# A layer-normed time-mix scan and a GELU feed-forward: the first block's splits move behind the second term of W1

## The chip, the cores and the metric

The kernel runs on one core of one Trainium2 chip. Its time is the device time of one execution in microseconds (us). A profile records one execution: when every instruction began, how long it took and what ended the idle time before it. Engines are named as the profile names them: PE is the matmul engine (PEld its weight loads), DVE the vector engine, ACT the scalar engine, POOL the general one, SP the queue that issues nearly all transfers (DMAs).

## The reference

The input `x` has 4 sequences of 1024 tokens and 512 channels. Every token is layer-normed, and two branches are added to the residual.

```python
xn = layernorm(x)
xx = concat([xn[:, 1:2], xn[:, :-1]], axis=1) - xn       # the token before, minus this one
k = einsum('btc,hc->bth', xn + xx * time_mix_k, Wk)      # 704 hidden
r = einsum('btc,hc->bth', xn + xx * time_mix_r, Wr)
w = exp(-exp(time_decay))
state_t = state_{t-1} * w + relu(k_t);  out_t = state_t * r_t
out = einsum('bth,ch->btc', out, Wv)                     # back to 512 channels
out = layernorm(out) * ln_gamma + ln_beta
D = gelu(float16(xn) @ W0.T + bias0).astype(float16)     # 2048 hidden
E = float16(D @ W1.T + bias1)
result = x + out + E
```

## The kernel before

**Blocks and chunks.** The 4096 tokens are cut into eight blocks of 512 (`blocks`, index `i`; the blocks 0, 1, ... of this text are that index, so "block 2" of the change's name is `i == 1`). For each block, a loop over `n` goes through 16 chunks of 128 hidden units of the feed-forward. In chunk `n`, `up` multiplies W0's rows for a chunk two ahead (PSUM tile `pd`), ACT applies the GELU (line 876) and a cast (line 879), and `down` multiplies chunk `n`'s `d` by W1's rows into four accumulators `pe` (line 888), one for each 128 tokens.

**Pieces.** Between chunks PE does pieces of the other branch: `three_pass` multiplies one 128-wide slice `h` of k or r (tiles `pa` at line 695, `pb` at line 446), `half_pass` and `raw_halves` the last 64 hidden units, `out_piece` the product with Wv. A piece leaves a follower, the work that takes its result out of PSUM (for `three_pass`: ACT's line 707, DVE's line 708, and then the scan, line 587, or the gate, line 604). Followers run in the next chunk. All tiles `pd`, `pa`, `pb` and the like share one pool of four PSUM banks (`ps_mm`, function `bank`): a matmul group that opens a bank must wait until the tile that held it has been read out.

**Splits.** PE takes a product in several terms: an operand is split into a high part and remainders. `split` (lines 199 and 200) does so for W0 and W1: ACT writes the high term, DVE the second. `split_x` (lines 278, 333, 335, 337) does it for the mixer's inputs, `split_kr` (278, 285, 294, 295, 296) for Wk and Wr, and `split_wv` (278, 312, 315 to 317, or 321 and 322 for the last half slice) for Wv. In each of the last three DVE masks, ACT copies the mask's result and DVE makes the remainders. `split_kr` also appends three stores of 256 KB to `stores`, and `split` for W1 two; `store_weights` hands them to SP at the end of a chunk. Splits are done once, in block 0 and the start of block 1; later blocks load what was stored.

**Block 0.** Here W1's rows are split as well: `load_w1` at the end of each chunk splits the rows of two chunks on, into tiles that have two buffers for the high term and three for the second. r's first slice and all of k's are made unsplit before the loop; r's slices 1 to 4 are `three_pass` pieces in chunks 3, 5, 7 and 9, and need r's split input (`first_xr`) and Wr's split slices.

**What sets the order.** DVE, ACT, PE and SP issue in the order that is written out (`manual_schedule`). Work put down with `put(n, ...)` goes into `bg[n]`, in the order in which it is put, and `woven` runs it in chunk `n` beside the followers. In block 0 a chunk's end is this:

```python
woven(works, jobs + bg[n])
if i == 0:
    waiting.append((d, load_w1(*nxt)))
```

`turn` stands for the DVE transposes of the next block's input (line 380), `stats` and `norm_apply` for its norm (354 and 358), `rounded` (line 835) for reading the four `pe` tiles out at a block's end; the next block's first `down` waits for that.

Of the kernel before, what the change touches and what calls it, by code (L numbers as in the profile page):

```python
# [22 lines left out]
def time_mix_and_gelu_ffn(  # L23
# [40 lines left out]
    Q = 32  # L64
    QS = 62
    RAW_OUT = 1
    WV_FIRST = {0: 12, 1: 13, 2: 15, 3: 15, 5: 15}
    S = 4096.0
    WS = 4096.0
    MASK = -4096  # L70
# [177 lines left out]
    def load_w1(i, n):  # L248
        name = f"w1_{i}_{n}"
        if i == LAST and n >= NN - 2:  # L250
            w1 = [part(f"{name}_0"), pair(f"{name}_1")[0]]
        else:
            w1 = [
                part(f"{name}_0", tag="w1", bufs=2),
                part(f"{name}_1", F16, tag="w1l", bufs=3),
            ]
        if i == 0:
            split(*w1, w1_raw.pop(n))
        for p in range(2):
            sbuf, kept = as_stored(w1[p], p), as_stored(w1_dram[n][p], p)  # L260
            if i == 0:
                stores.append((kept, sbuf))
            else:
                nc.sync.dma_start(sbuf, kept)
        return w1
# [696 lines left out]
    with tc.manual_schedule(engines=engines):  # L962
        for i in range(len(blocks)):
            j = i + 1
            tail = 4 if i == LAST else 0
            by_columns = range(NS // 2, NS) if tail else ()
            pieces, bg, early = defaultdict(list), defaultdict(list), defaultdict(list)

            def put(n, fn, *args, **home):
                bg[n].append(lambda: fn(*args, **home) if home else fn(*args))  # L970
# [32 lines left out]
            if i == 0:  # L1003
                state["x"] = x_next
                piece(1, raw_halves, i)
                for h in range(1, NF):
                    piece(2 * h + 1, three_pass, i, 1, h)
                for c in range(NC):
                    put(2 + c - (c == 0), split_w0, 2, c)
                    put(c // 2, load_w0, 3, c)  # L1010
                    put(5 + c, split_w0, 3, c)
                put(1, stats, *range(NS))
                put(3, lambda: norm_apply(j, state["x"]))
                for c in range(NC):
                    put(c // 2, split_first_xr, c)
                for n, h in ((7, 2), (10, 0), (11, 1)):
                    put(n, split_kr, 1, 0, h, **OWN)
                for h in range(1, NF):
                    put(2 * h - 1, first_kr, h)
                put(4, turn, 0, 1)  # L1020
                put(5, turn, 1, 5)
                put(7, turn, 5, 10)
                put(8, turn, 10, 11)
                put(9, turn, 11, 16)
                put(9, load_late_constants)
                put(12, split_half)
                for g in range(NN // G):
                    put(11 + (g or NN // G), store_w0l, g)
                put(15, store_weights)
                mix_at = (11, 12, 13, 15)  # L1030
            else:
                order = [(0, h) for h in range(NF)] + [(1, h) for h in range(NF)]
                halves_ahead_of = (3 if i == LAST else NF, NF)
                for k, (kind, h) in enumerate(order):
                    for half in range(2):
                        if k == halves_ahead_of[half]:
                            piece(half_at[half], half_pass, i, half)
                    piece(full_at[k], three_pass, i, kind, h)
                    if (kind, h) not in made:
                        put({(0, 3): 1, (0, 4): 2, (1, 0): 4}[kind, h], fetch_kr, i, kind, h)  # L1040
                    elif k > 1:
                        put(full_at[k - 2], fetch_kr, i, kind, h)
                xr_at = {1: (2, 3, 4, 5), LAST: (1, 2, 2, 3)}.get(i, (2, 2, 3, 3))
                for c, n in enumerate(xr_at):
                    put(n, split_xr, i, c)
                if j <= LAST:
                    put(2, fetch_x)
                    for s in range(NS):
                        put(3 + s // 2 if i == 1 else 4, stats, s)
                    put(5, lambda: norm_apply(j, state["x"]))  # L1050
                    turns = (4, 4, 4, 4) if i == 1 else (4, 5, 4, 3)
                    for k in range(sum(turns)):
                        unit = next(n for n in range(4) if k < sum(turns[: n + 1]))
                        put(6 + unit, turn, k, k + 1)
                mix_at = (10, 12, 13, 14)
# [3 lines left out]
            if j <= LAST:  # L1059
                for c in range(NC):  # L1060
                    put((10, 10, 11, 12)[c], x16, j, c)
                for c, n in enumerate(mix_at):
                    early[n].append((j, c))
                    put(n, mixed, j, c)
                    put(n + (n == 10), split_xk, j, c)
                for h, n in {0: WV_FIRST, 1: {NF - 1: 2}}.get(i, {}).items():
                    put(n, split_wv, h)
                put(13, fetch_kr, j, 0, 0)
                put(14, fetch_kr, j, 0, 1)

            pe = [ps_e.tile([P, C], F32, tag="pe", name=f"pe_{i}_{s}") for s in range(NS)]
            for n in range(NN):
                ahead = n + AHEAD
                if ahead == NN and j <= LAST:
                    xf = next_xf
                nxt = (i, ahead) if ahead < NN else (j, ahead - NN)
                paired = i > 0 and n < NN - tail
                order = HIGH_FIRST if paired and n % 2 == 0 else LOW_FIRST
                end = lambda s: NN - tail if s in by_columns else NN
                products, gelu = up(*nxt) if nxt[0] <= LAST else (None, None)  # L1080

                def hidden(p):
                    if products:
                        products(p, order if paired else HIGH_FIRST)

                def outputs(p):
                    if n < NN - tail:
                        down(n, range(NS), *operands, p, order, end=end)

                if n < NN - tail:  # L1090
                    operands = waiting.pop(0)
                if not paired:
                    hidden(0)
                    hidden(1)
                elif n % 2 == 0:
                    hidden(0)
                else:
                    hidden(1)
                    outputs(1)
                    hidden(0)  # L1100
                works = [follow() for follow in followers]
                works = [w for w in works if next(w, works) is None]
                several(scaled_now, *early[n])
                if i == 0 or n == out_at[0] or (n > out_at[0] and i < RAW_OUT):
                    finished(*works)
                    works = []
                followers = []
                if behind_works:
                    waiting.append(behind_works.pop()())
                if gelu and not paired:  # L1110
                    d = gelu()
                if ahead + 1 == NN and j <= LAST:
                    next_xf = ffn_input(j)
                if not paired:
                    outputs(1)
                outputs(0)
                if gelu and i > 0:
                    w1 = load_w1(*nxt)
                    if not paired:
                        waiting.append((d, w1))  # L1120
                two_on = (i, ahead + 2) if ahead + 2 < NN else (j, ahead + 2 - NN)
                if two_on[0] <= LAST:
                    load_w0l(*two_on)
                jobs = [
                    lambda s=s: finish(i - 1, s, e16s[s])
                    for s in (2 * n, 2 * n + 1)
                    if s < len(e16s)
                ]
                for work, *args in pieces[n]:
                    followers.append(work(*args))  # L1130
                if i == 0 and ahead + 2 < NN:
                    load_w1_raw(ahead + 2)
                woven(works, jobs + bg[n])
                if i == 0:
                    waiting.append((d, load_w1(*nxt)))
                elif paired and n % 2 == 0:
                    hidden(1)
                    outputs(1)
                    behind_works.append(lambda gelu=gelu, w1=w1: (gelu(), w1))
                elif paired:  # L1140
                    waiting.append((gelu(), w1))
                store_weights()
# [66 lines left out]
```

## Time and profile before

| | us |
|---|---|
| median of 3 runs | 857.76 (857.33 to 857.89) |
| the profiled execution | 857.93 |
| its span, first to last instruction | 856.1 |
| PE busy in the span | 847.0 (99%) |
| DVE busy | 687.1 (80%) |
| ACT busy | 438.1 (51%) |
| mean granted PE clock | 0.999 |

The profiled execution lies 0.17 us over the median, and 1.8 us of it are outside the span. A row of the timeline gives the start, the length, the engine, the line, the tile written and read, and in brackets the idle time before it and what ended that. A length is longer than the distance to the next row where two instructions overlap: DVE's split instructions last 0.69 us and start 0.61 us apart. The list of waits gives, for an engine and a line, the total idle time, how often it happened, and the longest.

### The profile page before, as it was taken

The numbers are of one execution on the slowest core, as the hardware profiler recorded it, in microseconds if no ns is written. First come the engines' busy times: TensorE is split into PE (matmuls) and PEld (weight loads), VectorE is DVE, ScalarE is ACT, GpSimd is POOL, SyncE is SP. The second block draws the span as 40 slices with busy tenths as digits, with TensorE's granted clock in tenths as the row PEclk, the third lists the DMA queues.
The fourth block names the chain that finished last, engine by engine and source line by source line (L and its number), as shares of the span: only waits on it lengthen the run. The fifth ranks groups of instructions, "written<-read, shape, count | busy, mean of one in ns | idle before, by whom it ended". The sixth has DMA issues, their size and how long they took to land.

```text
span 856.1 us, 11350 instructions
## 1 busy us (share of the span) xinstructions
PE 847.0 (99%) x3772; PEld 595.2 (70%) x3772; DVE 687.1 (80%) x1130; ACT 438.1 (51%) x748; POOL 80.4 (9%) x145
## 2 busy tenths in 40 slices
PE   9999999999999999999999999999999999999998
PEld 8556646667767767667777667677777667676776
DVE  6789898999868988789786897778796897876446
ACT  5857665546534563445725455344653545634422
POOL 1210000000211001000021001100011200200012
PEclk9999999999999999999999999999999999999999
DMA  9756995745467544856358455594465755467513
GB/s 279 252 178 239 306 282 193 249 151 182 148 230 225 172 136 149 288 165 209 130 170 284 148 180 172 159 308 146 151 193 161 272 173 181 127 220 247 169 54 111
DMA packets 120902, 166.72 MB, mean 195 GB/s; under 512 B 21487, under 2 KB 57740, under 8 KB 120844
## 3 DMA queue, kind: packets, MB, share of 16 engines
q1 hardware_dynamic: 120396, 165.34, 60.4%
q8 instruction: 30, 0.49, 0.2%
q10 hardware_dynamic: 448, 0.66, 0.2%
q14 instruction: 28, 0.23, 0.1%
HBM read 141.31 MB, written 24.64 MB: 194 GB/s over the span
## 4 chain that ended last, share of the span: by engine, by line
PE 82%; DVE 7%; DMA 5%; ACT 2%; issue 2%; SPq 2%; DVEq 0%; ACTq 0%
PE pd L862 22%; PE pe L888 22%; PE pa L695 14%; PE oa L792 7%; PE pb L446 7%; PE ob L800 4%; PE ph L724 3%; DMA x<-in_L_attn_x 2%; PE ob L802 1%; DMA krd<-wt 1%; DMA w0raw<-in_L_ffn_W 1%; SPq L239 1%; DVE w0l L200 1%; DVE wd L285 1%; ACT w L199 1%
## 5 line engine op out<-in xcount | busy, mean ns | idle before, releaser
L888 PE MATMUL pe<-w,d 128*128 128x512 f32 (+1 forms) x1008 | 262.9, 389 | 3.8 <-DVE w L200 3.4
L862 PE MATMUL pd<-xf,w0h 128*128 128x512 f32 x512 | 150.8, 415 | 0.1
L862 PE MATMUL pd<-x,w0l 128*128 128x512 f16 x512 | 132.2, 381 | 0.0
L876 ACT ACTIVATE d<-pd,late_sb 128x512 f16<-128x512 f32 x128 | 87.2, 681 | 75.4 <-PE pe L888 47.4
L862 PEld LDWEIGHTS pd<-xf,w0h 128*128 128x128 f32 x512 | 96.2, 188 | 28.4 <-issue 2.8
L888 PEld LDWEIGHTS pe<-w,d 128*128 128x128 f32 x504 | 94.7, 188 | 23.6 <-DVE e L835 1.2
L708 DVE SCALAR_TENSOR_TENSOR y<-pb,a 128x512 f32<-128x512 f32 x74 | 50.9, 688 | 65.5 <-PE pb L446 54.8
L888 PEld LDWEIGHTS <-d 128*128 128x128 f16 x524 | 50.6, 98 | 64.1 <-issue 5.1
L862 PEld LDWEIGHTS <-w0l 128*128 128x128 f16 x512 | 44.1, 98 | 62.2 <-issue 16.1
L879 ACT CAST d<-d 128x512 fp32r<-128x512 f16 x128 | 79.4, 620 | 10.3 <-PE pe L888 6.3
L380 DVE STREAM_TRANSPOSE xnT<-x 32x512 f32<-32x512 f32 x112 | 78.6, 702 | 2.2
L707 ACT ACTIVATE a<-pa 128x512 f32<-128x512 f32 x74 | 44.1, 596 | 70.2 <-PE pa L695 70.2
L348 POOL TENSOR_SCALAR ry<-mvy 128x1 f32<-128x1 f32 x32 | 18.9, 591 | 460.5 <-DVE mvy L355 460.5
L792 PE MATMUL oa<-wv,hg 128*128 128x512 f32 x140 | 54.5, 389 | 0.0
L792 PE MATMUL oa<-wv,lg 128*128 128x512 f32 x140 | 54.5, 389 | 0.0
L695 PE MATMUL pa<-lr,kr 128*128 128x512 f32 x136 | 52.9, 389 | 0.0
L695 PE MATMUL pa<-hr,kr 128*128 128x512 f32 x136 | 52.9, 389 | 0.0
L695 PE MATMUL pa<-hk,kr 128*128 128x512 f32 x132 | 51.4, 390 | 0.0
L695 PE MATMUL pa<-lk,kr 128*128 128x512 f32 x132 | 51.4, 389 | 0.0
L710 ACT ACTIVATE y<-y 128x512 f32<-128x512 f32 x35 | 22.1, 631 | 53.7 <-DVE y L708 53.7
L333 ACT CAST hg<-ug 128x512 fp32r<-128x512 f32 x35 | 21.7, 620 | 37.1 <-DVE ug L278 37.1
L807 DVE SCALAR_TENSOR_TENSOR oy<-ob,oa 128x512 f32<-128x512 f32 x28 | 19.3, 688 | 25.8 <-PE ob L802 25.8
(175 smaller groups left out, 1411.2 us busy)
## 6 DMA issues: line engine op xcount, KB each, us to landing
kr<-krd SPq DMA_DIRECT2D x201, 256.0 KB, 4.4
w<-w1d SPq DMA_DIRECT2D x112, 256.0 KB, 2.8
w<-w1d SPq DMA_DIRECT2D x112, 128.0 KB, 2.7
w0l<-w0d SPq DMA_DIRECT2D x108, 128.0 KB, 3.5
xres<-in_L_attn_x SPq DMA_DIRECT2D x32, 256.0 KB, 4.7
x<-in_L_attn_x SPq DMA_DIRECT2D x31, 256.0 KB, 5.0
krd<-wt SPq DMA_DIRECT2D x30, 256.0 KB, 3.3
out<-xres SPq DMA_DIRECT2D x28, 256.0 KB, 3.6
```

Of the source, the lines that this page charges most:

```text
L380: nc.vector.transpose(dst[i * Q : (i + 1) * Q, :, :, j, :], src[j * Q : (j + 1) * Q, :, :, i, :],)
L446: return nc.tensor.matmul(dst, w[:, c, :], src, start=(c == 0), stop=(c == NC - 1))
L695: nc.tensor.matmul(pa, w[p][:, c, :], xs[j, c][p], start=(c == 0 and p == 0), stop=(c == NC - 1 and p == 1),)
L707: nc.scalar.activation(a, pa, AF.Copy, scale=1.0 + 1.0 / S)
L708: nc.vector.scalar_tensor_tensor(y, pb, -1.0 / S, a, ALU.mult, ALU.add)
L724: nc.tensor.matmul(pa, w[:, c].rearrange("p two k -> p (two k)"), xs[j, c][p], start=(c == 0 and p == 0), stop=(c == NC - 1 and p == 1),)
L792: nc.tensor.matmul(pa, gs[i, h][p][:, cols], wv[h][p], start=(h == 0 and p == 0), stop=(h == NF - 1 and p == 1),)
L800: nc.tensor.matmul(pb, gs[i, h][2][:, cols], wv[h][2], start=(h == 0), stop=False)
L862: nc.tensor.matmul(pd, weights(c, p), src[c][p], start=(c == 0 and p == order[0]), stop=(c == NC - 1 and p == order[1]),)
L876: nc.scalar.activation(d16, pd, AF.Gelu, bias=b0_sb[:, n : n + 1], scale=1.0 / WS)
L879: nc.scalar.copy(d, d16)
L888: nc.tensor.matmul((sums or pe)[s], d[p][:, s * P : (s + 1) * P], w1[p][:, cols], start=(n == first and p == order[0]), stop=(n == end(s) ...
```

## The change

Nothing is added or taken out; work is put elsewhere. In block 0, the splits of r's input (`split_first_xr`, chunks 0 and 1), of Wr's slices 1 to 4 (`first_kr`, chunks 1, 3, 5, 7) and of three slices of Wk (`split_kr`, chunks 7, 10, 11) leave `bg` for a list of their own, `behind_w1`, which is run after `load_w1`. So in its chunk each stands behind all other work, W1's split included, where it stood before W1's split and, but for chunks 7 and later, ahead of what was put after it. In chunk 7 the order of Wr's slice 4 and Wk's slice 2 is also turned round. The half slice of Wv (`h == 5`) is split in chunk 3 of block 1, no longer in chunk 15 of block 0, and Wv's slice 4 in chunk 8 of block 1, no longer in chunk 2.

```diff
-    WV_FIRST = {0: 12, 1: 13, 2: 15, 3: 15, 5: 15}
+    WV_FIRST = {0: 12, 1: 13, 2: 15, 3: 15}
...
             pieces, bg, early = defaultdict(list), defaultdict(list), defaultdict(list)
+            behind_w1 = defaultdict(list)
...
                 for c in range(NC):
-                    put(c // 2, split_first_xr, c)
+                    behind_w1[c // 2].append(lambda c=c: finished(split_first_xr(c)))
+                for h in range(1, NF):
+                    behind_w1[2 * h - 1].append(lambda h=h: first_kr(h))
                 for n, h in ((7, 2), (10, 0), (11, 1)):
-                    put(n, split_kr, 1, 0, h, **OWN)
-                for h in range(1, NF):
-                    put(2 * h - 1, first_kr, h)
+                    behind_w1[n].append(lambda h=h: split_kr(1, 0, h, **OWN))
                 put(4, turn, 0, 1)
                 put(5, turn, 1, 5)
                 put(7, turn, 5, 10)
...
-                for h, n in {0: WV_FIRST, 1: {NF - 1: 2}}.get(i, {}).items():
+                for h, n in {0: WV_FIRST, 1: {NF: 3, NF - 1: 8}}.get(i, {}).items():
                     put(n, split_wv, h)
...
                 woven(works, jobs + bg[n])
                 if i == 0:
                     waiting.append((d, load_w1(*nxt)))
+                    for job in behind_w1[n]:
+                        job()
```

## The prediction

> **What bounds the kernel now.** I read the page first, then the waits, then the timelines of PE, DVE and ACT around each wait. The page's busy times and clock:
>
> ```profile
> PE 847.0 (99%) x3772; PEld 595.2 (70%) x3772; DVE 687.1 (80%) x1130; ACT 438.1 (51%) x748; POOL 80.4 (9%) x145
> ...
> PEclk9999999999999999999999999999999999999999
> ```
>
> PE is the bound over the whole span, so only time in which PE waits can be won, and each wait added is lost in full: from 160 us to the end the waits show none of PE on another engine, and none of its weight loads over 0.3 us, so a lag that PE has by then is a lag at the end. PE's waits on other engines in the list of waits:
>
> ```profile
> PE pe L888 <- DVE w L200: 3.4, 4, 1.7
> ...
> PE pa L695 <- ACT a L707: 0.4, 1, 0.4
> ```
>
> The 3.4 us are what the change is after. PE's timeline gives their places, chunks 3, 5, 7 and 9 of block 0:
>
> ```profile
> 52.16 1.95 PE L888 MATMUL pe<-w,d 128*128 128x512 f16 x8 [1.67 <-DVE w L200]
> ...
> 62.46 1.95 PE L888 MATMUL pe<-w,d 128*128 128x512 f16 x8 [0.26 <-DVE w L200]
> ...
> 73.05 1.94 PE L888 MATMUL pe<-w,d 128*128 128x512 f16 x8 [0.53 <-DVE w L200]
> ...
> 84.08 1.94 PE L888 MATMUL pe<-w,d 128*128 128x512 f16 x8 [0.99 <-DVE w L200]
> ```
>
> But DVE is nearly full there (7.79 us of the 8 from 84 to 92), and ACT stands in its queue for DVE. Chunk 7 on DVE, then on ACT:
>
> ```profile
> 77.84 0.42 DVE L278 TENSOR_SCALAR wu<-wr 128x512 int32<-128x512 int32 x1
> 78.29 0.69 DVE L285 TENSOR_TENSOR wd<-wr,wu 128x512 f32<-128x512 f32 x1
> 79.02 0.69 DVE L296 SCALAR_TENSOR_TENSOR wt<-wd,wu 128x512 fp32r<-128x512 f32 x1
> 79.74 3.56 DVE L380 STREAM_TRANSPOSE xnT<-x 32x512 f32<-32x512 f32 x5
> 83.33 0.69 DVE L200 SCALAR_TENSOR_TENSOR w<-w1raw,w 128x512 f16<-128x512 f32 x1
> ```
>
> ```profile
> 78.29 0.62 ACT L294 CAST wt<-wu 128x512 fp32r<-128x512 f32 x1 [0.37 <-DVE wu L278]
> 79.02 0.63 ACT L295 ACTIVATE wt<-wd 128x512 fp32r<-128x512 f32 x1
> 79.56 0.61 ACT L199 ACTIVATE w<-w1raw 128x512 fp32r<-128x512 f32 x1
> 80.07 0.58 ACT L707 ACTIVATE a<-pa 128x512 f32<-128x512 f32 x1
> 80.55 0.68 ACT L876 ACTIVATE d<-pd,late_sb 128x512 f16<-128x512 f32 x1
> ```
>
> Line 707 reads a bank out, line 876 too, and both stand behind ACT's two copies of a split, which wait for DVE's mask and remainder.
>
> **What the change moves.** No instruction comes or goes. Moved behind W1's split: four `split_x` (3 DVE, 1 ACT each) and seven `split_kr` (3 DVE, 2 ACT, 3 stores each); moved into block 1: Wv's half slice (2 DVE, 4 ACT); later in it: Wv's slice 4 (3 DVE, 2 ACT). W1's term now comes early, but the copies on ACT are masked last on DVE, and behind them stand the next chunk's line 707 and GELU.
>
> Three durations from rows: DVE takes 1.8 us for one split (47.19 to 49.05, 76.05 to 77.84); ACT's first copy starts 0.46 after DVE's mask does (49.05, 49.51), and the instruction behind its second copy 1.7 (49.05, 50.77). "Lag" is against the trace before.
>
> *Chunks 0 to 3.* ACT's W1 term for chunk 2 stands ahead of r's copies, but its buffer is read until chunk 0's product ends (35.77 + 1.95 = 37.72): done 38.4, DVE's term to 39.0, then r's two splits. Their second copy (41.3) holds the GELU of line 876: 41.85 for 39.56, and all that hangs on it, W0's split and the norm's statistics, lags 2.3. W1's term for chunk 3 is made at 47.6, before PE comes at 50.5: the 1.67 are gone. PE goes on to the first `pa`, at 52.3 for 53.95. That needs the bank which ACT's line 679 reads out; before it was queued at 51.29. Now it follows two r splits and Wr's: DVE masks at 48.2, 50.0, 51.9, line 679 is at 53.6, done 54.1. PE starts at 54.2: **lag 0.25**; the 1.67 gained are paid by a wait of 1.9.
>
> *Chunks 5 and 6.* ACT and DVE still lag 2.2. Wr's slice 2 is masked at 62.1 (59.35), line 707 comes at 63.85 (61.59), its bank is free at 64.45; PE arrives at 64.25 - 0.26 + 0.25 = 64.24. Lag 0.2. W0's high terms, two at 65.58, come 2.25 later, the second done at 69.0; PE's fourth `pd` matmul wanted it at 67.67. **Lag 1.35.** DVE's four transposes then end at 72.55, W1's term at 73.25, ahead of PE (73.9): the 0.53 go, lag 0.8.
>
> *Chunk 7.* Wr's slice 3 is masked at 73.2, line 707 at 74.9 (69.76, +5.1; PE needs its bank at 75.65, so it is just in time). GELU, W0's term (78.9) and DVE's (79.6 for 75.44) follow. Now the five transposes come ahead of the splits: to 83.8; W1's term to 84.5, PE at 83.9 waits 0.6 for 0.99: lag 0.45. Wr's slice 4 is masked at 84.4, Wk's at 86.2, line 707 comes at 87.95 for 80.07, its bank is free at 88.55. PE wants it at 85.86 + 0.45. **Lag 2.7.** This is the dearest step: the cover of line 707 was 4.2 us (done 80.65, wanted at 84.9 but for PE's own wait), and it slips 7.9.
>
> *Chunks 10 to 15.* DVE goes on with lag 4.9 (line 708 at 96.55 for 91.67), of which 1.54 of idle at 96.40 is used up; the mixer's scaled input on ACT (line 403) comes at 100.2 for 96.27 and, behind Wk's slice 1, at 106.7 for 101.84. DVE's chain from there to the block's end lags 4.0, and so do the casts of the next input (line 442, 116.0 for 112.00), which PE waits for already. **Lag 4.0.**
>
> *Block 0's end.* DVE's line 835 stood behind two DVE instructions of Wv's half (129.87 to 131.01). Without them it starts at 133.9, lag 2.9. PE's four matmuls that wait for it began 131.79 to 133.54, where 131.44 to 132.12 would have done; now the last starts at 136.45. **Lag 2.9**: a gain of 1.1 inside the loss.
>
> *Block 1.* In chunk 2 the wait of 0.6 goes (`pa` at 155.12; 154.52 without) with Wv's slice 4: lag 2.3. In chunk 3 DVE masks Wv's half after the second r split and two statistics: 161.2. ACT, which before went from r's copy straight to the GELU,
>
> ```profile
> 157.59 0.61 ACT L333 CAST hr<-ur 128x512 fp32r<-128x512 f32 x1
> 158.12 0.68 ACT L876 ACTIVATE d<-pd,late_sb 128x512 f16<-128x512 f32 x1
> ```
>
> waits for that mask, makes four copies (130.33 to 133.05, 2.7 us) and is at the GELU at 164.35, done 165.05. PE wants the bank at 159.79 + 2.3 = 162.1. **Lag 5.3.** In chunk 8 Wv's slice 4 is masked behind four transposes, the last two at 188.88 before. With DVE 5 late that is 195.3; line 707 of r's slice 1 follows at 197.0 for 186.53, done 197.6; PE wants the bank at 191.17 + 5.3 = 196.5. **Lag 6.5.**
>
> The sum: +6.5 on the profiled 857.93 gives 864.4; that execution lies 0.17 over the median, so 864.3 against 857.76.
>
> **What I cost at nothing.** SP: the 21 stores of the splits now follow W1's two in a chunk. Behind them on SP stands the load of W1 rows two chunks ahead (about 7 us of cover, 3.3 to land), and Wk's slices 0 and 1, which are read back from 111.85 on (stored from 96.97); 5 us more are covered. W1's buffers in chunk 11: ACT's write for chunk 13 must wait for a store that SP issues behind seven loads; it was issued at 94.39, median 3.5 us to land, and can be 2.2 later, 101.6, where ACT comes at 103.7. If DMA, full from 92 to 124 us (share 1.0), makes that cover fail, 0 to +1. The PE clock: the trace shows 0.999 with a longest wait of 1.7 us; mine are up to 3.0. By that row the clock stays. [...]
>
> **Rivals.**
> - *The waits go and nothing takes their place (faster).* PE wins 3.4 in block 0, 1.1 at its end, 0.6 in block 1: 852.6. It decides at chunk 7: line 707 would have to begin by 83.8, 3.7 later than now. For it: PE's own row for line 707 has one wait, 0.4 us, in the whole span. Against: five transposes (3.56) and W1's term stand ahead of that split in DVE's written order, and 3.56 + 0.61 + the 2.3 of lag exceed 3.7.
> - *Block 0 pays, block 1 has slack (slower, less).* Lag 2.3 to 3: 860.4. It takes the GELU behind Wv's four copies to have 5.5 us of room; its row (158.12, PE at 159.79) shows 1.
> - *More than my sum.* The hand-offs that I round down, the store above, and lags that meet: 7.5 to 9.5, 866.
> - *No change.* The four waits won (3.4) and the end's 1.1 pay chunk 7 and the casts, and block 1 has room: within 0.2%, which is about what a measurement of this kernel can tell.
>
> **The numbers.** Likeliest, slower by 5 to 7.5: 0.62. Slower by 2 to 5: 0.17. By more than 7.5: 0.12. Within 0.2% (1.7 us): 0.04. Faster: 0.05. Range 860.5 to 867.2: it takes in the second case's middle and most of the third, and leaves out about 0.2. Predicted 864.3.
>
> **What would show it.** The row "PE pe L888 <- DVE w L200" falls from 3.4 to about 0.6, at chunk 9 alone; in its place PE (or its weight loads) waits for ACT's lines 679, 707 and 876 at the first `pa` of r's slices 1 (1.9) and 4 (2.2), and of block 1's k slice 4 (3.0) and r slice 2 (1.1). ACT's largest waits become line 294 and 321 on DVE's masks. I am wrong if line 707 in chunk 8 comes within 3 us of 80.07, or if the `pa` after Wv's half starts with no wait.

## The result and the profile after

The changed kernel takes 866.88 us (median of 4 runs, 865.80 to 868.21) where the kernel before, measured beside it, took 857.83: +9.05 us, a ratio of 1.0107 with a 95% interval of 1.0088 to 1.0126. The forecast was 864.3 in a range of 860.5 to 867.2. Sign and place were right; of the cases priced ahead it is "more than my sum" (0.12), not the likeliest.

The profiled execution took 868.21 us, its span 866.4. From the page, PE's busy row and the granted clock, where the sixth slice (108 to 130 us) shows the one digit that is not a 9:

```profile
PE 850.7 (98%) x3772; PEld 597.6 (69%) x3772; DVE 687.9 (79%) x1130; ACT 437.3 (50%) x748; POOL 80.8 (9%) x145
...
PEclk9999989999999999999999999999999999999999
```

PE is still the bound and does the same 3772 matmuls, in 3.7 us more of busy time (850.7 for 847.0) and 6.6 us more of idle time. The list of PE's waits (total, times, longest):

```profile
PE pa L695 <- ACT a L707: 3.4, 2, 2.0
PE pd L862 <- ACT xf L442: 2.6, 1, 2.6
PE pa L695 <- ACT kr L679: 2.0, 1, 2.0
PE pa L695 <- ACT d L876: 1.6, 1, 1.6
PE pd L862 <- ACT w0h L199: 0.9, 1, 0.9
PE idle L463 <- PEq L1195: 0.8, 1, 0.8
PE pe L888 <- DVE w L200: 0.7, 1, 0.7
```

The row that the change is after fell from 3.4 us in four places to 0.7 in one. Five rows of ACT, 10.5 us together, stand in its place; before, ACT's rows made 0.4. PE now waits little for W1's terms, and mostly for banks that ACT has not read out and for operands that ACT has not copied.

The places, on PE's timeline: chunk 3's first `pa`, chunk 9's W1 product (the only one of the four waits that is left) and its first `pa`, and the next input's product:

```profile
54.99 0.50 PE L695 MATMUL pa<-hr,wt 128*128 128x512 f32 x1 [1.96 <-ACT kr L679]
...
85.51 1.95 PE L888 MATMUL pe<-w,d 128*128 128x512 f16 x8 [0.67 <-DVE w L200]
89.51 0.50 PE L695 MATMUL pa<-hr,wt 128*128 128x512 f32 x1 [2.05 <-ACT a L707]
...
119.12 2.36 PE L862 MATMUL pd<-xf,w0h 128*128 128x512 f32 x4 [2.61 <-ACT xf L442]
```

Why chunk 9's `pa` waits is seen on ACT's timeline in chunk 8, to be read against the same rows before, where line 707 stood at 80.07:

```profile
80.34 0.62 ACT L199 ACTIVATE w<-w1raw 128x512 fp32r<-128x512 f32 x1
85.83 0.62 ACT L294 CAST wt<-wu 128x512 fp32r<-128x512 f32 x1 [4.87 <-DVE wu L278]
86.56 0.63 ACT L295 ACTIVATE wt<-wd 128x512 fp32r<-128x512 f32 x1
87.62 0.62 ACT L294 CAST wt<-wu 128x512 fp32r<-128x512 f32 x1 [0.43 <-DVE wu L278]
88.35 0.63 ACT L295 ACTIVATE wt<-wd 128x512 fp32r<-128x512 f32 x1
88.88 0.58 ACT L707 ACTIVATE a<-pa 128x512 f32<-128x512 f32 x1
```

ACT is done with W1's high term, then stands idle for 4.87 us in front of a copy whose mask DVE makes only after five transposes (81.17 to 84.73) and W1's term. Line 707 has nothing to do with that mask, but is behind the copies in ACT's order, and begins 8.8 us later than before (8.0 if the start's 0.85, explained below, is taken off; the forecast had 7.9).

Two things more are in this trace. ACT's write of W1's high term in chunk 11 waits for a store, and the clock of PE halves after the wait for `xf`. ACT's timeline, and the stretches from 116 to 128 us (busy time of PE, PEld, DVE, ACT and POOL, then PE's clock, DMA share, GB/s):

```profile
106.05 0.63 ACT L199 ACTIVATE w<-w1raw 128x512 fp32r<-128x512 f32 x1 [1.16 <-DMA w1d<-w]
```

```profile
116.00:120.00 4.00, 1.39 (x10) 0.58 (x2) 3.62 (x6) 3.97 (x8) 0.00 (x0) 0.85 1.00 286
120.00:124.00 4.00, 4.00 (x10) 1.66 (x10) 3.19 (x6) 3.44 (x8) 0.00 (x0) 0.50 1.03 292
124.00:128.00 4.00, 4.00 (x12) 2.36 (x11) 3.83 (x9) 1.82 (x3) 1.58 (x4) 0.80 0.85 259
```

From 118.8 to 125.6 us the clock is at 0.50, and matmuls start 0.43 us apart where 0.22 is usual. In the kernel before, no such stretch is found between the first 5 us and the last 2.

### The profile page after: what moved, and what is told of

Read it like the earlier page. It is cut to its first block, busy times and chain, and to the rows that moved or that the text cites. A ratio compares the mean times of both kernels' runs of the same rounds, so it can differ in the third digit from the quotient of the medians.

```text
span 866.4 us, 11348 instructions
## 1 busy us (share of the span) xinstructions
PE 850.7 (98%) x3772; PEld 597.6 (69%) x3772; DVE 687.9 (79%) x1130; ACT 437.3 (50%) x748; POOL 80.8 (9%) x145
## 4 chain that ended last, share of the span: by engine, by line
PE 87%; DVE 6%; ACT 3%; DMA 3%; issue 1%; SPq 0%; DVEq 0%; ACTq 0%
PE pd L862 24%; PE pe L888 23%; PE pa L695 14%; PE oa L792 7%; PE pb L446 7%; PE ob L800 4%; PE ph L724 3%; PE pk L446 2%; PE ob L802 1%; DVE xnT L380 1%; PE po L751 1%; DMA w1d<-w 1%; DMA krd<-wt 1%; ACT d L876 1%; DMA wvraw<-in_L_attn_Wv 1%
## 5 line engine op out<-in xcount | busy, mean ns | idle before, releaser
L333 ACT CAST hr<-ur 128x512 fp32r<-128x512 f32 x32 | 19.8, 620 | 39.0 <-DVE ur L278 39.0
```

## The experiments

"Lag" is again the start of a PE matmul less that of the same matmul in the trace before, with places named by their time before. Each reading takes off what lag a trace has already at its start, ahead of all moved work, where the clock reaches its full rate at different times (matmuls of 128 columns start 0.21 us apart until 9.6 us in the changed kernel's trace and until 4.9 before, 0.11 later on). For the changed kernel 0.85 us are taken off; the lag there is 0.91 at 10 us and 0.77 from 13 us on. The other traces start with lags between 1.15 (the next run) and -0.4.

**The two halves of the change.** First r's and the mixer's splits alone, Wv's split places as before:

```diff
-    WV_FIRST = {0: 12, 1: 13, 2: 15, 3: 15}
+    WV_FIRST = {0: 12, 1: 13, 2: 15, 3: 15, 5: 15}
...
-                for h, n in {0: WV_FIRST, 1: {NF: 3, NF - 1: 8}}.get(i, {}).items():
+                for h, n in {0: WV_FIRST, 1: {NF - 1: 2}}.get(i, {}).items():
```

> Only the splits of block 0 move; Wv's splits stay where they were. Theory A (ACT's copies wait for DVE masks that now stand behind the transposes and W1's term, and PE waits for the PSUM banks and casts queued behind them): PE lags as in the changed kernel up to block 0's end, 5.6 us and 2.3 more where the clock halves; the gain of 1.1 at the block's end and the losses of 2.5 and 1.2 in block 1 are absent; time 857.8 + 5.6 = 863.4, or 865.7 with the half clock. Theory B (Wv's moves are the loss): 857.8 or less.

Measured: 863.89 us (863.00 to 864.64), ratio 1.0067 (1.0052 to 1.0082). Up to 112.67 the lags are those of the changed kernel (5.6 us there), the waits the same (707: 2.5, `xf`: 2.5, 679: 2.0), and a half clock of 3.4 us follows at 119.4.

Then Wv's places alone, the kernel before with the two lines above as changed:

> Only Wv's splits move (half slice to chunk 3, slice 4 to chunk 8 of block 1); block 0 is as before. Theory A: PE gains about 1.1 at block 0's end and 0.6 to 1.0 in chunk 2 of block 1, then waits about 3 for the GELU behind the half slice's four ACT copies and 1.2 behind slice 4: 857.8 + 2.3 = 860.1. With the 5.6 (or 7.9) of the splits alone that adds up to the 8.0 and 10.2 of the changed kernel's two groups of runs. Theory B (the move of Wv is nearly all): 865. Theory C (it has no cost of its own, DVE's lag made it one): 856 to 857.

Measured: 860.79 us (860.75 to 862.25), ratio 1.0039 (1.0025 to 1.0053). PE has gained 1.2 us by block 0's end and has a lead of 1.9 us in chunk 2 of block 1. Then comes one wait that takes it all and more, from the list of waits and PE's timeline:

```profile
PE pa L695 <- ACT d L876: 2.9, 1, 2.9
```

```profile
160.78 0.65 PE L695 MATMUL pa<-hk,wt 128*128 128x512 f32 x1 [2.90 <-ACT d L876]
```

That matmul lasts 0.65 us where 0.50 is usual after a wait: the clock is at one half from 161.0 to 164.4 us and takes another 1.7. The slice in chunk 8 costs nothing here, since PE, 2.9 us late, finds that bank read out. By their ratios the two halves cost 5.7 and 3.3 us of 857.8, together about the whole loss. That they add up so well is in part chance, since the steps differ: in the changed kernel the wait at the half slice is 1.6 us for 2.9 and no half clock follows it, the half clock behind `xf` costs 2.35 for 0.9 with the splits alone, and slice 4 costs 1.6 where Wv's move alone paid nothing for it.

**Is it the transposes?** In chunks 5 and 7 the transposes now stand ahead of the splits on DVE. They are put behind them:

```diff
-                put(5, turn, 1, 5)
-                put(7, turn, 5, 10)
+                behind_w1[5].append(lambda: turn(1, 5))
+                behind_w1[7].append(lambda: turn(5, 10))
```

> As the changed kernel, but the transposes of chunks 5 and 7 too stand behind W1's split and behind the moved splits, so that the splits are again ahead of them on DVE. Theory A: the wait for line 707 in chunk 9 (2.05 us) and the 0.9 in chunk 6 go or shrink below 0.6, the wait for the casts shrinks, the clock stays at full: 857.8 + 4 = 861.8 (860.5 to 863). If the transposes were not what ACT's copies wait for, 866 to 867 as the changed kernel.

Measured: 863.35 us (863.01 to 863.84), ratio 1.0061 (1.0046 to 1.0076). PE's list of waits:

```profile
PE pd L862 <- ACT xf L442: 2.4, 1, 2.4
PE pa L695 <- ACT kr L679: 2.0, 1, 2.0
PE pa L695 <- ACT d L876: 1.8, 1, 1.8
...
PE pe L888 <- DVE w L200: 0.2, 1, 0.2
```

The waits for line 707 are gone and those for W1's term down to 0.2; at 84.08 PE leads by 0.3 us, at 93.96 it is level (0.1), where the changed kernel lags 3.0. So the dearest step of the forecast is shown to be what it said, a read-out behind copies that wait for DVE behind transposes. The wait of 0.9 for W0's high term in chunk 6 is absent too, but that is not shown to be the transposes: PE comes there late by a half clock, and the last run below, with the transposes behind and no half clock, still has it. The wait for `xf` stays at 2.4 (a step of 2.46 at 112.67), and in the profile the clock halves three times for 3.4 us, after waits of 2.0 (line 679), 2.4 (`xf`) and 1.8 (line 876), at 1.7, 1.35 and 1.7 us.

**The store of W1.** The changed kernel with three buffers for W1's high term in place of two (one tile less in the pool of `QS` pays for the memory), so that ACT's write for chunk 13 finds one free:

```diff
-    QS = 62
+    QS = 61
...
-                part(f"{name}_0", tag="w1", bufs=2),
+                part(f"{name}_0", tag="w1", bufs=3),
```

> As the changed kernel, but W1's high term has three buffers, not two (and the general pool one tile less, 61 for 62). Theory A: ACT's wait of 1.16 for the store of W1 in chunk 11 goes, the first wait for r's slice (2.0) falls by 0.5, PE's wait for the casts falls from 2.6 to about 1.2 and the clock does not halve: 857.8 + 6.7 = 864.5 in every run, against 865.8 and 868.0. If the stores have no part in it: 866 to 867.

Measured: 865.02 us (864.83 to 866.07), ratio 1.0083 (1.0068 to 1.0098). ACT's row has no wait any more, and PE's wait for `xf` falls from 2.61 to 1.21:

```profile
104.66 0.63 ACT L199 ACTIVATE w<-w1raw 128x512 fp32r<-128x512 f32 x1
```

```profile
117.59 2.31 PE L862 MATMUL pd<-xf,w0h 128*128 128x512 f32 x4 [1.21 <-ACT xf L442]
```

So the store cost 1.4 us there. The lag at 112.67 is 3.9, close to the forecast's 4.0. The half clock is still there for 3.4 us, after the shorter wait (four `f16` matmuls then take 1.93 us, where the kernel before has 1.04).

**The clock by itself.** The changed kernel with eight matmuls added ahead of block 1's first product, into the bank that this product then overwrites, to keep PE busy while `xf` is made:

```diff
+            if (i, n) == (1, 0) and p == order[0]:
+                for _ in range(8):
+                    nc.tensor.matmul(pd, w0h[0, 0][:, :P], w0h[1, 0], start=True, stop=True)
```

> As the changed kernel, but PE does eight more matmuls into the bank of block 1's first chunk while it waits for the casts; the first real product overwrites them. If a PE idle of over 3 us is what halves the clock: no half clock in the profile, every run near 865.5 to 866 (8.0 over before), none at 868. If the slow stretch has another cause (the DMA load there, the matmuls' operands): the matmuls of 121 to 126 us still start 0.43 us apart and some runs are at 868.

Measured: 866.86 us (866.22 to 868.31), ratio 1.0108 (1.0094 to 1.0122). No half clock follows at 119 us, so the wait ahead of it, 2.61 us in the changed kernel and 0.30 here, is what brings that one; that a wait must be over 3 us is not shown. But PE then comes earlier to the GELU of block 1's chunk 3, waits 2.9 us there for 1.6 (line 876, which is 879 in this kernel), and the clock halves after that wait instead (166.0 to 169.4, 1.5 us). The expectation failed: nothing is won. Nor do the runs order by clock: this kernel took 866.22 us at a mean clock of 0.994 and 868.31 at 1.000, the kernel with the transposes behind 863.07 at 0.993 and 863.01 at 1.000.

**Wv's slice 4 alone.** The kernel before, with this slice in chunk 8 of block 1 and the half slice where it was:

> The kernel before with one move alone: Wv's slice 4 from chunk 2 to chunk 8 of block 1; the half slice stays in block 0. Theory A (where DVE has no lag, chunk 8 has room): the wait at the third k slice (0.4 to 0.6) and the small ones beside it go and nothing takes their place: 857.8 - 0.6 to - 1.1 = 856.7 to 857.2. If the place in chunk 8 itself costs the 1.6 that the changed kernel shows there: 858.8.

Measured: 857.14 us (856.64 to 858.95, 11 runs), ratio 0.9996 (0.9987 to 1.0004): no difference that can be told. The wait of 0.6 us in chunk 2 of block 1 is gone, the profiled execution leads by 0.8 us, and no other step shows.

**Room for Wv's slices.** The kernel before with slice 0 in chunk 13, 1 in 15 of block 0, and 3 and 4 in chunk 10 of block 1:

```diff
-    WV_FIRST = {0: 12, 1: 13, 2: 15, 3: 15, 5: 15}
+    WV_FIRST = {0: 13, 1: 15, 2: 15, 5: 15}
...
-                for h, n in {0: WV_FIRST, 1: {NF - 1: 2}}.get(i, {}).items():
+                for h, n in {0: WV_FIRST, 1: {3: 10, NF - 1: 10}}.get(i, {}).items():
```

> The kernel before with Wv's splits spread otherwise: slice 0 one chunk later (13), slice 1 in 15, slices 3 and 4 in chunk 10 of block 1. Theory A (DVE and ACT pace block 0's end, and block 1's chunk 10 has room): PE's four waits for the casts at 113 us shrink by 1.8 in all, DVE's reading out of the accumulators comes 1.8 earlier, the wait in chunk 2 of block 1 goes, and 1.5 is lost behind the two splits in chunk 10: 857.8 - 2 = 855.8 (855 to 857). If block 0 is paced by PE alone: 857.8 or more.

Measured: 856.05 us (855.95 to 857.11, 11 runs), ratio 0.9981 (0.9972 to 0.9990). It beats both kernels. The lead is 0.9 us behind the next input's product, 2.35 at block 0's end and 3.1 in chunk 2 of block 1; a new wait of 1.2 us at 210 (`oa` for ACT's line 333) and what follows leave 1.7.

**Copies apart from masks.** The step at the half slice could come from the row of ACT behind DVE's masks, or from four more ACT copies in full chunks. In this kernel only Wv moves, to the changed kernel's places, but DVE's two passes stand in chunk 3 and ACT's copies two in chunk 4 and two in chunk 5 (with tiles of their own for what they read):

```diff
...
+                if i == 1:
+                    put(4, copy_wv_half, 0)
+                    put(5, copy_wv_half, 1)
```

> Only Wv's splits are moved, as in the changed kernel with its two new places in block 1 (the half slice in chunk 3, slice 4 in chunk 8), but the half slice is taken apart: VectorE's mask and difference stand in chunk 3, ScalarE's four copies two in chunk 4 and two in chunk 5, when what they read is long there. With slice and copies together this move gave 860.8 us: TensorE ran up to 2.06 us ahead of the kernel before until it waited 2.9 us for the GELU of block 1's chunk 3 and then lost 1.6 us to the halved clock. Theory A (it is the row of ScalarE behind VectorE's two passes that holds the GELU): the wait of 2.9 falls under 1 us, no halved clock follows, the lead of about 2 us is kept to the end, and the time is 855.5 to 856.5 us. Theory B (these chunks have no room for four more ScalarE copies, wherever they stand): the wait only moves one or two chunks on, at 1.5 to 3 us, and the time is 858.5 to 861 us.

Measured: 857.45 us (857.07 to 857.89, 11 runs), ratio 0.9992 (0.9983 to 1.0001), against 860.79 with copies and masks together. On the half slice the first theory holds: the wait of 2.9 us is gone, no half clock follows, and the lead of 1.9 us is kept past chunks 4 to 7. Its time was missed, because that lead then meets slice 4 in chunk 8, which was hidden as long as PE was late. PE's timeline (the lines of this kernel lie 11 further down, so 706 is 695, and 718 is 707):

```profile
190.55 0.50 PE L706 MATMUL pa<-hr,kr 128*128 128x512 f32 x1 [1.23 <-ACT a L718]
```

**Both together:** the spread of the kernel at 856.05 (slices 0, 1 and 2 in chunks 13, 15 and 15 of block 0, 3 and 4 in chunk 10 of block 1) and the half slice as in the run above.

> The version that the runs so far point to: the kernel before with Wv's splits alone moved, slice 0 to chunk 13 and slices 1 and 2 to chunk 15 of block 0, slices 3 and 4 to chunk 10 of block 1, and the half slice in block 1 with VectorE's part in chunk 3 and ScalarE's copies in chunks 4 and 5. Without the half slice's move this gave 856.05 us. If theory A of the run beside it holds, block 0 ends another 1 to 2 us earlier and the time is 854.3 to 855.6 us; if theory B holds, the wait in chunks 4 to 6 of block 1 gives that back and the time is 856 to 859 us.

Measured: 856.96 us (856.66 to 857.55, 11 runs), ratio 0.9989 (0.9979 to 0.9998). A miss: no more than the spread alone. The lead at 155.92 is 3.1 us, the same as with the spread, and 2.5 of it go between 203 and 211 (707's wait 0.6, `oa`'s 1.3).

**The changed kernel twice more**, for the clock of its runs:

> The changed kernel again, for its clock. Its runs stood in two groups about 2.1 us apart (865.8 and 868), and the profiled one, at 868.2, had the granted clock at one half for 6.8 us from 118.8 us on, which cost 2.35 us. If that stretch is what parts the groups, a run near 865.8 shows it at 3.4 us or not at all, and a run near 868 shows 6.8 us. If both groups show the same stretch, something else parts them.

> The same as the run ahead of it, once more: a stretch of half clock of 3.4 us or none near 865.8 us, of 6.8 us near 868 us.

Measured: 867.53 and 868.44 us, both at a mean clock of 0.996, as in the profiled execution above with its 6.8 us of half clock, and the same waits (2.6 and 2.9 for `xf`, the largest difference). They differ by the lag of the first microseconds. Neither fell near 865.8, and the four runs first measured had 0.996, 0.996, 0.998 and 0.998 at 868.21, 865.80, 867.87 and 865.88 us. So the half clock is not shown to be what parts them.

**All answers at once.** The changed kernel, its splits still behind W1's term, with the transposes behind as well, three buffers for W1's high term, the half slice's copies apart, and slice 4 in chunk 10.

> The changed kernel with an answer to each loss that the runs have named, all of them together: the transposes of chunks 5 and 7 of block 0 also behind W1's second term (this took the waits of 2.0 us in chunks 7 and 9 away), a third buffer for W1's high term (the wait for xf fell from 2.6 to 1.2), Wv's half slice taken apart as in wv_copies (the step at chunk 4 of block 1 went), and slice 4 in chunk 10 of block 1 instead of chunk 8 (where it cost 1.2 to 1.5 us). What the change is for, splitting r's input and kernels behind W1's second term, stays. If the list is whole, the lag before the next input's product at 112.67 is about 1 us, the end of block 0 takes 1.2 off and chunk 2 of block 1 another 0.6, and the kernel is at 856.5 to 858.5 us, within 0.2% of the kernel before, or up to 1.5 us more where a wait of about 2 us for r's slice 1 (L679) still halves the clock. If the losses don't add, and the moved splits cost ScalarE's or VectorE's time wherever the other work stands, it stays at 860 us or more.

Measured: 858.29 us (857.99 to 859.39, 11 runs) beside 858.62 for the kernel before, ratio 1.0001 (0.9992 to 1.0010): the loss of 9 us is gone. Its list of waits:

```profile
PE pa L706 <- ACT kr L690: 1.5, 1, 1.5
PE oa L803 <- ACT hg L344: 1.3, 1, 1.3
PE pd L873 <- ACT xf L453: 1.2, 1, 1.2
PE pd L873 <- ACT w0h L199: 0.9, 1, 0.9
```

The lag at 112.67 is 0.8 (expected: about 1), -0.4 at block 0's end, -1.1 in chunk 2 of block 1, 0.4 after 210. The row for line 200 is no longer among its waits of 0.3 us or more, and the clock does not halve between the start and the end. The list of losses is whole to within what can be told, though not every loss is gone: what is left is paid by the waits for W1's term that are won and by what Wv's moves give back. The change's own aim, 3.4 us of waits, is met; in its place stand four other waits of 4.9 us together.

## Why the prediction was right, and where its terms were off

What the profiled execution lost, place by place, less the 0.85 us of its start:

| place | lag forecast | lag measured |
|---|---|---|
| chunk 3, first `pa` (53.95) | 0.25 | 0.19 |
| W0's high term in chunk 6 (67.67) | 1.35 | 1.30 |
| chunk 9, W1's product (84.08) | 0.45 | 0.58 |
| chunk 9, first `pa` (85.86) | 2.7 | 2.8 |
| next input's product (112.67) | 4.0 | 5.6 |
| behind the half clock (116.77) | 4.0 | 7.95 |
| block 0's end (134.12) | 2.9 | 6.6 |
| block 1, after slice 4's wait in chunk 2 (155.12) | 2.3 | 5.95 |
| after the half slice (159.79) | 5.3 | 7.5 |
| after slice 4 in chunk 8 (191.17), to the end | 6.5 | 9.3 |

**Chunks 0 to 9** went as worked out to 0.13 us: waits of 1.96 and 2.05 us for 1.9 and 2.2, 0.67 for 0.6. The way of working, each moved split in DVE's order, ACT's copies behind it, and the read-out behind these, is shown by the run with the transposes behind, where that step alone is taken away.

**Chunks 10 to 15** is the first term that was mis-sized, 5.6 for 4.0. It was "costed at nothing": the store of W1 that holds ACT's write, given as 0 to +1. The cover failed: 1.16 us on ACT's row, 1.4 us on PE's wait by the run with three buffers. Both of its parts were too small. SP issued that store at 99.79 (94.39 before), 5.4 us later (4.5 without the start's 0.85) where 2.2 were allowed, and it took 6.2 us to land, where the forecast used the median of 3.5 over the whole span; the same store before had taken 5.5.

**The clock** is the second, left out of the sum. The forecast read from a longest wait of 1.7 us without a fall that the clock would stay for its own waits of up to 3.0; no row showed that. In this trace the wait of 2.61 us was followed by 6.8 us at half rate, worth 2.35 in lag. With three buffers the fall followed a wait of 1.21, while single waits of 1.96 and 2.05 us in the changed kernel's trace had none, so by the measurement the length of a single wait does not decide it. Most stretches of 3.4 us at half rate cost 1.35 to 1.7 us of lag; with the splits alone it was 0.9, since that stretch begins with the four `xf` matmuls, which start 0.52 us apart in the kernel before too.

**Block 0's end and chunk 2 of block 1** gave back 1.2 and 0.6 to 0.8, as worked out (1.1 and 0.6).

**Block 1's half slice** is the third, 1.6 for 3.0, and its cause is shown on both sides: PE came 3.65 us later than the forecast had it (5.95 for 2.3), while ACT's GELU, at 167.44 for 164.35, was only 2.25 later once the 0.85 of the start is taken off; the difference of 1.4 is what the wait was shorter by. ACT's and PE's rows in the changed kernel:

```profile
164.78 0.63 ACT L321 ACTIVATE wv<-vu 64x512 fp32r<-64x512 f32 x1 [2.84 <-DVE vu L278]
...
167.44 0.69 ACT L876 ACTIVATE d<-pd,late_sb 128x512 f16<-128x512 f32 x1
```

```profile
168.18 0.50 PE L695 MATMUL pa<-hk,wt 128*128 128x512 f32 x1 [1.56 <-ACT d L876]
```

With PE early, in the kernel with Wv's move alone, the same wait was 2.9. Slice 4 in chunk 8 cost 1.6 for 1.2 (a wait of 1.39); nothing where PE was late (Wv's move alone) and 1.23 where it was early.

The steps add to 9.4 us in the profiled execution, 10.3 with the start. Against the 6.5 of the forecast stand 1.6 more at the casts, 2.35 of the clock, 0.4 at slice 4, and 1.4 less at the half slice: 2.9. That execution lies 1.3 us over the median, and the median 2.6 over the forecast. What a half clock is worth in the median stays open, since the times of one kernel's runs do not follow their mean clock; so does what parts runs at 865.8 from those at 868. The median lies 0.3 us inside the range's upper end, and that is partly luck: two of the four runs (867.87 and 868.21) and both later ones (867.53 and 868.44) lie above it, and three terms that were too small were partly paid by one that was too large.

Of the rivals, "block 1 has slack" falls with the wait of 1.6 (2.9 with Wv's move alone). "The waits go and nothing takes their place" falls with line 707 at 88.88, 8.8 us later, where it allowed 3.7. "No change" falls with the ratio, though it describes the mended kernel well.

## What to carry to other kernels

Where an engine works in order, a split that is moved on one engine moves what stands behind its copies on the next: ask for each moved copy which bank read-out follows it in the queue and how long its cover is, not only what the moved work itself is needed for. Four ACT copies behind DVE's masks cost 3 us of wait in front of a GELU, and none when they were put a chunk later than their masks. And a buffer whose store is said to be covered in a stretch where the DMA share is 1.0 should be given its price in the sum, since it was the first cover to fail.

## What had not been expected of the hardware

PE's clock fell to one half after single waits of 1.2 to 2.9 us, in stretches of 3.4 us (6.8 in the changed kernel's trace) that each added 0.9 to 1.7 us of lag (2.35 for the long one), and not after others of 1.67 (before), 1.96 and 2.05 us (after) or 1.5 (the last run). The wait of 2.0 us for line 679 was followed by a fall with the transposes behind (clock 0.50 from 54.3 to 57.7) and by none in the changed kernel. With the wait filled by other matmuls, the fall came after the next wait instead.

Two traces, read over their whole spans, suggest that it also counts where a wait lies. In the changed kernel's the clock changes at 9.56, 118.78, 125.61 and 866.30 us, which is 32, 2 and 217 times 3.413 us apart; before, at 4.88 and 854.80, 249 times. With the transposes behind, the falls near 54.3, 115.7 and 163.5 are 18 and 14 of them apart. Counted in stretches of 3.413 us from these points (the first 14 us and the end left out), the changed kernel's PE is idle for 2.27 us in the stretch ahead of the fall at 118.78 and for at most 1.56 in any other; before, the most is 1.67, and no fall follows. The wait of 1.96 us for line 679, which no fall followed, is cut at 53.93 into 0.9 and 1.06. The run with three buffers, where the fall came after a wait of 1.21, speaks against an idle time that decides alone. No run was made to test any of this. Also, runs of one kernel at mean clocks of 0.993 and 1.000 took the same 863.0 us; why the lost cycles don't show there is open.
